# A graph attention layer with routed experts on one core: three expert tiles are turned by VectorE instead of TensorE, and the opening does its steps in another order

## The chip, the core and the metric

The kernel runs on one core of one Trainium2 chip. The core has five engines that each work through a queue of their own: TensorE (PE; its weight loads are listed apart as PEld), VectorE (DVE), ScalarE (ACT), GpSimd (POOL) and SyncE (SP), which here issues most of the transfers. Transfers themselves are moved by 16 DMA engines. Data lies in SBUF, products of TensorE land in PSUM banks, and inputs and outputs lie in device memory (HBM). The metric is device time in microseconds (us) for one run of the whole kernel. The median of three runs of the kernel before is 1252.25 us, from 1250.95 to 1253.42.

## The reference

All numbers are 32-bit floats; there are N = 4096 rows of D = 256 features, 4 heads of 64 columns, and 8 experts with 1024 hidden columns.

```python
def gnn(x, adj, W, a1, a2, Wr, br, gamma, beta):      # x is layernorm(x)
    h = einsum('nd,hdk->hnk', x, W)
    s_col = einsum('hnk,hk->hn', h, a1)
    s_row = einsum('hnk,hk->hn', h, a2)
    e = leaky_relu(s_row[:, :, None] + s_col[:, None, :], 0.2)
    att = softmax(where(adj > 0, e, -9e15), axis=-1)   # 4096 x 4096, four heads
    out = heads_side_by_side(einsum('hij,hjk->hik', att, h))
    y = elu(out) + x @ Wr + br
    return gamma * (y - mean(y)) / sqrt(var(y) + 1e-5) + beta

def ffn(x, Wg, bg, W1, b1, W2, b2):                    # x is layernorm(x)
    top_w, top_i = top_k(x @ Wg + bg, 2)
    share = softmax(top_w)                             # of the two experts chosen
    return sum(share[e] * (gelu(x @ W1[e] + b1[e]) @ W2[e] + b2[e])
               for the two experts e of each row)

x = x + gnn(layernorm(x), adj, ...)
x = x + ffn(layernorm(x), ...)
```

## The kernel before

**Attention.** Rows are held in blocks of 512 (four row tiles of 128 each). The attention runs over four row ranges of 1024 rows; in each, a loop over 32 column tiles `j` loads a tile of the transposed adjacency (`load_mask`), builds four heads' weights on VectorE (line 1703, tile `w`) and lets TensorE multiply them with the projected rows `ha` (line 1204, `acc`) and add them up (line 1213, `den`). In the first row range the projections of later blocks are made along the way.

**The opening** (`first_phase`, line 917) makes block 0 and 1 ready and starts the first columns while only the first half of the range is there. Its order is written out by hand: `in_trace_order` (line 819) ties every instruction to the one before it on its engine, so each engine works through the opening exactly in the order of the program text. Rows are centred on ScalarE (`centred`, line 839) from the means that `moments_of` (line 833) finds on VectorE, and are turned by TensorE, two row tiles at a time, in `turned_pair` (line 905: four transposes into one PSUM bank, then one copy to `turned[b]`). `weights_turned` (line 667) turns the heads' weights `wall` on TensorE and copies them on ScalarE to `wT`. `heads_made` (line 638) turns the vectors a1 and a2 on TensorE and spreads them on VectorE to `heads`. `scores_weights` (line 678) multiplies the two (`pw`) and copies the result into the last columns of `wall` (line 687), so that the projections `product_of` (line 897) give heads and scores at once. `squares_of_weights` and `limits_found` (lines 689 and 695) find a bound on the scores; `root_steps` (line 166) takes the inverse root of the variances in eleven short VectorE instructions. `rest_of_loads` (line 650) is seven loads issued by GpSimd, of which the first waits for the moments that it is given. `warm_up` (line 744) is matmuls on constants. All small PSUM results take turns in three banks (`bank`, line 245), and tiles of the tag `large` in three buffers.

**The experts.** During the attention of the later row ranges each finished row is routed: it is written, 260 floats wide (256 features, two shares, the row's number, the first choice), to the place of each of its two experts in `lists` in device memory. Expert tiles of up to 256 rows of one expert are then taken from these lists. The plan has 9 `early` and 8 `mid` tiles, which take rows of the first three row ranges, eight `final` ones with up to 512 rows, and two more; `todo` (line 2003) is their order. The main loop (line 2029) does for tile i, on TensorE in this order: the up products of tile i (`up`, line 1878, with gelu on ScalarE), a step of the last row block's own work (`between`, line 1989), the turn of tile i+1 (`turn`, line 1858), the down products of tile i (`down`, line 1900). The order on TensorE is fixed by `queue` (line 533). `fetch` (line 1791) issues on SyncE what a tile needs: rows, second bias, first and second weights (1 MB each, two buffers).

Rows come in one of two forms. The first NEAR tiles are **near**: `load_rows_of` (line 572) loads 256 whole rows of 260 floats in one transfer, ahead of time, and `turn_rows_of` (line 607) turns them with four TensorE transposes and two copies from PSUM. All others are loaded in **blocks**: `load_blocks_of` (line 583) issues one small transfer for the last four floats of each row (`known`) and eight for blocks of 32 rows by 32 columns, laid so that one VectorE instruction, which transposes every 32 by 32 block by itself (line 1871), gives the turned tile. Tile 0 is loaded and turned during the attention; tiles 1 to 5 have the buffers `early`.

The instructions' order in the queues outside of the hand-ordered parts is made by a planner that follows the program order, apart from what is ready much earlier.

Of the kernel before, what the change touches and what calls it, by code (L numbers as in the profile page):

```python
# [38 lines left out]
def over_partitions(vec, n):  # L39

    return bass.AP(tensor=vec.tensor, offset=vec.offset, ap=[[0, P], [1, n]])
# [3 lines left out]
def gat_then_moe(  # L45
# [19 lines left out]
    nc = tc.nc  # L65
    N, D = x.shape
    H, _, K = W.shape
    E, _, F = W1.shape
# [11 lines left out]
    MID = BOTH - EARLY  # L80
    LATE = 2 * N // TT - BOTH
    SURE = 2
    NEAR = 6
    KT = -(-N // TT)
    LAG = 6

# [2 lines left out]
    TB = B // P  # L89
# [76 lines left out]
    def root_steps(var, v, r, n, part=1.0, steps=3, sign=1):  # L166

        nc.vector.tensor_scalar(v, var, part, EPS, op0=OP.mult, op1=OP.add)
        yield
        nc.vector.tensor_scalar(  # L170
            r.bitcast(I32), v.bitcast(I32), -0.5, 1597463007.0, op0=OP.mult, op1=OP.add
        )
        yield
        for i in range(steps):
            way = sign if i + 1 == steps else 1
            q = small.tile([P, n], F32, tag="q", name="q")
            nc.vector.tensor_tensor(q, r, r, OP.mult)
            yield
            nc.vector.scalar_tensor_tensor(q, q, -0.5 * way, v, op0=OP.mult, op1=OP.mult)
            yield  # L180
            nc.vector.scalar_tensor_tensor(r, q, 1.5 * way, r, op0=OP.add, op1=OP.mult)
            yield
# [36 lines left out]
    def forward(apart, stack):  # L219
# [25 lines left out]
        def bank(shape, name):  # L245
            return ps.tile(shape, F32, tag="bank", name=name, bufs=3)
# [300 lines left out]
        def order_of(ins):  # L547

            if ordered[0] or strict[0]:
                queue(ins)  # L550
            return ins.ins
# [67 lines left out]
        with ExitStack() as layer:  # L619
# [30 lines left out]
            def rest_of_loads(behind=None):  # L650

                ins = nc.gpsimd.dma_start(wr, Wr.rearrange("(c p) d -> p c d", p=P)).ins
                if behind is not None:
                    after(ins, behind, "the first rows are loaded first")
                nc.gpsimd.dma_start(brm, over_partitions(br, D))
                nc.gpsimd.dma_start(wg[:, :, :E], Wg.rearrange("(c p) e -> p c e", p=P))
                nc.gpsimd.dma_start(bgb, over_partitions(bg, E))
                nc.gpsimd.dma_start(gam, over_partitions(gamma, D))
                nc.gpsimd.dma_start(bet, over_partitions(beta, D))
                nc.gpsimd.dma_start(b1r, b1.rearrange("e (c p) -> (e c) p", p=P))  # L660
# [6 lines left out]
            def weights_turned():  # L667

                pt = bank([P, 2, DC, P], "ptw")
                for i in range(2):  # L670
                    for c in range(DC):
                        order_of(nc.tensor.transpose(pt[:, i, c], wall[:, c, ts(i, P)], ident))
                wT = large("wT").rearrange("p t d -> p (t d)")[:, : 2 * DC * P]
                wT = wT.rearrange("p (i c d) -> p i c d", i=2, c=DC)
                nc.scalar.copy(wT, pt)
                return wT

            def scores_weights(wT):

                pw = bank([P, DC, 2 * H], "pw")  # L680
                for c in range(DC):
                    for i in range(2):
                        order_of(nc.tensor.matmul(
                            pw[:, c], wT[:, i, c], heads[:, i].rearrange("p s h -> p (s h)"),
                            start=(i == 0), stop=(i == 1),
                        ))
                nc.vector.tensor_copy(wall[:, :, HK:], pw)

            def squares_of_weights():

                sq = gat.tile([P, DC, H], F32)
                nc.vector.tensor_tensor(sq, wall[:, :, HK : HK + H], wall[:, :, HK : HK + H], OP.mult)
                return sq

            def limits_found(sq):

                pl = bank([P, H], "plim")
                for c in range(DC):
                    order_of(nc.tensor.matmul(
                        pl, all1f, sq[:, c, :], start=(c == 0), stop=(c == DC - 1)  # L700
                    ))
                v, r = (gat.tile([P, H], F32, name=name) for name in ("vlim", "rlim"))
                yield from root_steps(pl, v, r, H, 1.09 * D, steps=0)
                nc.vector.scalar_tensor_tensor(limits[:, :H], v, -1.0, r, op0=OP.mult, op1=OP.mult)
                yield
                nc.vector.tensor_tensor(limit, v, r, OP.mult)
                yield
# [125 lines left out]
            def moments_of(xb, mv, t):  # L833

                st = small.tile([P, 6], F32, tag="st", name="st")
                nc.vector.bn_stats(st, xb[:, t, :])
                return nc.vector.bn_aggr(mv[:, t, :], st).ins

            def centred(xb, mv, t):

                nc.scalar.activation(
                    xb[:, t, :], xb[:, t, :], AF.Identity, bias=mv[:, t, 0:1], scale=-1.0
                )
# [58 lines left out]
                        start=(c == 0), stop=(c == DC - 1),  # L902
                    ))

            def turned_pair(xb, b, t0, copy):

                pt = bank([P, DC, 2, P], "pt")
                for k in range(2):
                    for c in range(DC):
                        order_of(nc.tensor.transpose(pt[:, c, k], xb[:, t0 + k, ts(c, P)], ident))  # L910
                copy(turned[b][:, :, t0 * P : (t0 + 2) * P], pt.rearrange("p c k i -> p c (k i)"))

            def room_turned(b):
# [3 lines left out]
            def first_phase(weigh, norms):  # L917

                nc.scalar.activation(warm, tiny, AF.Exp)
                first = rows_loaded(0)  # L920
                mvs = [small.tile([P, TB, 2], F32, tag="mv", name="mv") for b in range(HB)]
                rs = [gat.tile([P, TB], F32, name=f"rrow{b}") for b in range(HB)]
                vs = [gat.tile([P, TB], F32, name=f"vrow{b}") for b in range(HB)]
# [3 lines left out]
                for t in range(2):  # L927
                    seen = moments_of(first, mvs[0], t)
                    centred(first, mvs[0], t)
                adj = load_adj(gat, range(R), 0, 1, 3)  # L930
                after(marks["adj"], seen, "the first rows and weights are loaded first")
                second = rows_loaded(1)
# [2 lines left out]
                    nc.sync.dma_start(first_adj[:, k], adjT[ts(2 + k, P), :R])  # L935
                fetched[2] = rows_loaded(2)
                room_turned(0)
                turned_pair(first, 0, 0, nc.vector.tensor_copy)
                wT = weights_turned()
                rest_of_loads(moments_of(first, mvs[0], 2))  # L940
                heads_made()
                warm_up(1)
                moments_of(first, mvs[0], 3)
                for t in range(2, TB):
                    centred(first, mvs[0], t)
                scores_weights(wT)
                turned_pair(first, 0, 2, nc.scalar.copy)
                sq = squares_of_weights()
                phs = [projected(t) for t in range(TB)]
                product_of(0, 0, phs[0])  # L950
                limit_steps = limits_found(sq)
                roots = root_steps(mvs[0][:, :, 1], vs[0], rs[0], TB, sign=-1)
                for _ in range(6):
                    next(roots)
                for _ in roots:
                    next(limit_steps, None)
                for _ in limit_steps:
                    pass
                for t in range(1, TB):
                    product_of(0, t, phs[t])  # L960
# [24 lines left out]
                roots = root_steps(mvs[1][:, :, 1], vs[1], rs[1], TB, sign=-1)  # L985
# [201 lines left out]
            def load_adj(pool, rows, j, n, bufs):  # L1187

                at = pool.tile([P, n, len(rows)], I32, tag="adj", name="adj", bufs=bufs)
                marks["adj"] = nc.sync.dma_start(  # L1190
                    at,
                    adjT[j * P : (j + n) * P, rows.start : rows.stop].rearrange(
                        "(t p) i -> p t i", p=P
                    ),
                ).ins
                return at
# [594 lines left out]
        def fetch(t, i):  # L1791
# [3 lines left out]
            chosen = t is early or t is mid  # L1795
            near = chosen and i + EARLY * (t is mid) < NEAR
            if near:
# [218 lines left out]
        def load_full(i):  # L2016
            xr = work.tile([CH, 2, RW], F32, tag="early", name="early", bufs=NEAR - 1)
            load_rows_of(early, i, xr)
            full_rows.append(xr)

        for i in range(1, NEAR):
            load_full(i)
            if i in (1, 4):
                jobs.append(fetch(*todo[len(jobs)]))
            if i in (1, 2):
                given.append(loads_of(b0 + i - 1, (residuals, large)[i - 1]))
# [64 lines left out]
    with tc.If(held(1, 1) > 0):  # L2091
        further()
        with tc.If(held(2, 1) > 0):
            with ExitStack() as again:
                held, further, rest_of_sums, _ = forward(False, again)
# [37 lines left out]
```

## Time and profile before

| | |
|---|---|
| median of three runs | 1252.25 us |
| the profiled execution | 1252.34 us |
| its span, first to last instruction | 1250.3 us |
| first weights of the attention (line 1703) begin | 16.6 us |
| attention's last product, first expert product | 775 us |
| expert tiles 0 to 5 | 775 to 862 us |
| last expert product ends | 1242 us |

The profile is of one execution. Times of instructions are counted from the start of the span. A row of a chain or a timeline gives the start, the duration, the engine, the tile that is written, the line, and how many instructions were joined; what stands in square brackets is the idle time of the engine before it and what ended it. Rows of a window give, after the stretch and its length, the busy time of TensorE, its weight loads, VectorE, ScalarE and GpSimd with the number of instructions in brackets, then TensorE's granted clock (1.00 is full), the busy share of the DMA engines, and GB/s. "SPq" is SyncE's queue issuing a transfer; the name of a line can be that of a helper.

### The profile page before, as it was taken

The numbers are of one execution on the slowest core, as the hardware profiler recorded it, in microseconds if no ns is written. First come the engines' busy times: TensorE is split into PE (matmuls) and PEld (weight loads), VectorE is DVE, ScalarE is ACT, GpSimd is POOL, SyncE is SP. The second block draws the span as 40 slices with busy tenths as digits, with TensorE's granted clock in tenths as the row PEclk, the third lists the DMA queues.
The fourth block names the chain that finished last, engine by engine and source line by source line (L and its number), as shares of the span: only waits on it lengthen the run. The fifth ranks groups of instructions, "written<-read, shape, count | busy, mean of one in ns | idle before, by whom it ended". The sixth has DMA issues, their size and how long they took to land.

```text
span 1250.3 us, 22717 instructions
## 1 busy us (share of the span) xinstructions
PE 1235.8 (99%) x8874; PEld 647.2 (52%) x8874; DVE 845.5 (68%) x1566; ACT 448.6 (36%) x918; POOL 242.1 (19%) x217
## 2 busy tenths in 40 slices
PE   9999999999999999999999999999999999999997
PEld 5444444332233332332324324888888876666686
DVE  6999887889999989999999996855111211111110
ACT  4332322165522375322655321533323332222322
POOL 4000000001002601006110015124432212222222
PEclk9999999999999999999999999999999999999999
DMA  6343433436533646335366322968889897555562
GB/s 216 107 131 118 158 114 102 145 126 147 177 113 105 224 116 202 104 101 157 115 164 199 119 81 100 274 167 228 218 244 250 193 234 149 109 135 114 133 164 31
DMA packets 155540, 190.22 MB, mean 152 GB/s; under 512 B 72312, under 2 KB 125680, under 8 KB 155040
## 3 DMA queue, kind: packets, MB, share of 16 engines
q1 hardware_dynamic: 133392, 145.39, 40.2%
q0 software_dynamic: 20544, 36.74, 13.3%
q10 hardware_dynamic: 1488, 6.55, 1.4%
q8 instruction: 71, 1.16, 0.4%
q14 instruction: 45, 0.37, 0.1%
HBM read 155.77 MB, written 29.74 MB: 148 GB/s over the span
## 4 chain that ended last, share of the span: by engine, by line
PE 94%; DVE 3%; issue 1%; DMA 1%; ACT 1%; POOLq 0%; SPq 0%; DVEq 0%; ACTq 0%
PE acc L1204 34%; PE po L1921 18%; PE ph L1887 17%; PE den L1213 17%; PE pr L1059 2%; DVE w L1703 2%; PE ph L1107 2%; PE acc L900 1%; PE ptx L1259 0%; DMA early<-lists 0%; PE pt L784 0%; PE ptr L1505 0%; PE po L1960 0%; PE pl L1270 0%; DMA xb<-in_x 0%
## 5 line engine op out<-in xcount | busy, mean ns | idle before, releaser
L1204 PE MATMUL acc<-w,ha 128*32 128x512 f32 x4096 | 669.7, 593 | 0.8 <-DVE w L1703 0.8
L1703 DVE SCALAR_TENSOR_TENSOR w<-er,eb,am 128x1024 f32<-128x1024 f32 x496 | 606.5, 1277 | 27.2 <-PE den L1213 27.2
L1213 PE MATMUL den<-w,unit 128*2 128x512 f32 x2048 | 466.5, 592 | 0.1
L1204 PEld LDWEIGHTS acc<-w,ha 128*32 128x32 f32 x4096 | 184.3, 110 | 291.4 <-issue 253.3
L1620 ACT ACTIVATE am<-adj 128x1024 bf16<-128x1024 int32 x124 | 130.7, 1054 | 352.5 <-DVE w L1703 194.3
L1887 PE MATMUL ph<-xT,w 128*128 128x256 f32 (+5 forms) x864 | 229.9, 423 | 0.2 <-ACT hT L1891 0.2
L1921 PE MATMUL po<-w,hT 128*128 128x256 f32 (+1 forms) x1040 | 229.7, 379 | 0.0
L1891 ACT ACTIVATE hT<-ph,bias 128x256 f32<-128x256 f32 (+5 forms) x216 | 111.4, 518 | 287.7 <-issue 181.6
L1921 PEld LDWEIGHTS po<-w,hT 128*128 128x128 f32 (+1 forms) x1040 | 195.7, 189 | 31.2 <-issue 3.4
L1887 PEld LDWEIGHTS ph<-xT,w 128*128 128x128 f32 x864 | 163.4, 190 | 59.8 <-issue 38.0
L1213 PEld LDWEIGHTS den<-w,unit 128*2 128x2 f32 x2048 | 93.6, 85 | 148.1 <-issue 139.1
L1946 POOL DMA_INDIRECT out<-o,ids x66 | 102.8, 1558 | 323.5 <-DMA out<-o,ids 144.1
L1934 DVE SCALAR_TENSOR_TENSOR o<-po,share,b2s 128x256 f32<-128x256 f32 (+2 forms) x66 | 31.6, 479 | 194.1 <-PE po L1921 167.5
L1390 POOL DMA_INDIRECT lists<-xe,at x64 | 89.2, 1394 | 267.3 <-issue 183.7
L1871 DVE STREAM_TRANSPOSE xT<-xr 128x512 f32<-128x512 f32 (+5 forms) x21 | 17.9, 851 | 87.5 <-DMA xr<-lists 42.3
L1059 PE MATMUL pr<-wr,xT 128*128 128x256 f32 x128 | 30.4, 381 | 0.2 <-ACT er L1153 0.2
L1909 ACT ACTIVATE b2s<-b2b,share 128x256 f32<-128x256 f32 x68 | 30.0, 498 | 0.0
L1127 POOL DMA_DIRECT2D residual<-rb x6 | 4.7, 786 | 122.1 <-DVE rb L1074 90.7
L1455 POOL DMA_DIRECT2D xf<-in_x x6 | 8.1, 1347 | 100.3 <-ACT xf L1454 100.3
L1059 PEld LDWEIGHTS pr<-wr,xT 128*128 128x128 f32 x128 | 24.1, 190 | 5.4 <-issue 0.9
L1107 PE MATMUL ph<-wall,xT 128*128 128x264 f32 x96 | 24.6, 399 | 0.0
L207 ACT ACTIVATE m<-y,off 128x256 f32<-128x256 f32 x48 | 23.7, 494 | 1.1 <-DVE off L215 0.6
(394 smaller groups left out, 617.3 us busy)
## 6 DMA issues: line engine op xcount, KB each, us to landing
adj<-in_adj SPq DMA_DIRECT2D x126, 512.0 KB
w<-in_L_ffn_W SPq DMA_DIRECT2D x54, 1024.0 KB
er<-parts ACTq DMA_DIRECT2D x3, 2048.0 KB
lists<-zeros POOLq DMA_DIRECT2D x8, 520.0 KB
residual<-rb POOLq DMA_DIRECT2D x8, 512.0 KB
rb<-residual SPq DMA_DIRECT2D x8, 512.0 KB
out<-y POOLq DMA_DIRECT2D x8, 512.0 KB
xb<-in_x SPq DMA_DIRECT2D x7, 512.0 KB
```

The source lines that it names most:

```text
L1059: order_of(nc.tensor.matmul(pr[:, k, :], turned[b][:, c, ts(t0 + k, P)], wr[:, c, :], start=(c == 0), stop=(c == DC - 1),))
L1107: order_of(nc.tensor.matmul(phs[t - t0], xT[:, c, ts(t, P)], wall[:, c, :], start=(c == 0), stop=(c == DC - 1),))
L1204: queue(nc.tensor.matmul(acc[half][h // 2][here : here + Q, :], ha[:, j, h * K + g * Q : h * K + (g + 1) * Q], w[half][h], start=(j == 0), ...
L1213: queue(nc.tensor.matmul(den[here : here + HB, :], unit[:, j, h, 1 - half : 1 - half + HB], w[half][h], start=(j == 0 and half == 0), stop ...
L1390: ins = nc.gpsimd.indirect_dma_start(lists, bass.IndirectOffsetOnAxis(ap=at[:, k, t : t + 1], axis=0), xe[:, t, :], None,).ins
L1620: nc.scalar.activation(am, at, AF.Relu, scale=2.0)
L1703: marks["w"] = nc.vector.scalar_tensor_tensor(wh[:, these], er[:, these, h], eb[:, j, h : h + 1], mask[:, these], op0=OP.max, op1=OP.min,).ins
L1887: order_of(nc.tensor.matmul(ph, job["w1"][:, c, ts(f, P)], xT[:, c, :], start=(c == 0), stop=(c == DC - 1),))
L1891: job["gelu"] = nc.scalar.activation(hT[:, f, :], ph, AF.Gelu, bias=job["bias"][:, f : f + 1]).ins
L1921: order_of(nc.tensor.matmul(po[:size], hT[:, f, k * CH : k * CH + size], w2[:, f, :], start=(f == 0), stop=(f == FC - 1),))
L1934: given_out.append(nc.vector.scalar_tensor_tensor(o[:size], po[:size], share[:size, k : k + 1], b2s[k][:size], op0=OP.mult, op1=OP.add,).ins)
L1946: added.append(add().ins)
```

## The change

Two parts. First, NEAR goes from 6 to 3: only tiles 0, 1 and 2 are near, and tiles 3, 4 and 5 come in blocks and are turned by VectorE like those behind them. The buffers `early` go from five to two, three row loads vanish, and the fetch of tile 2 moves ahead of the last block's second set of loads.

Second, the opening is put in another order. The heads' weights are turned ahead of the first pair of row tiles; the moments of row tiles 2 and 3 and the GpSimd loads come ahead of the adjacency loads in the text; `turned_pair` is split into `pair_turned` (TensorE) and `pair_kept` (the copy), so that the copy of the first pair comes behind `heads` on VectorE; two root steps follow it, and the other nine run behind the squares instead of between the steps of the limits.

```diff
-    NEAR = 6
+    NEAR = 3
...
+            def pair_turned(xb, b, t0):
                 pt = bank([P, DC, 2, P], "pt")
                 for k in range(2):
                     for c in range(DC):
                         order_of(nc.tensor.transpose(pt[:, c, k], xb[:, t0 + k, ts(c, P)], ident))
+                return pt
+
+            def turned_pair(xb, b, t0, copy):
+                pair_kept(pair_turned(xb, b, t0), b, t0, copy)
+
+            def pair_kept(pt, b, t0, copy):
                 copy(turned[b][:, :, t0 * P : (t0 + 2) * P], pt.rearrange("p c k i -> p c (k i)"))
...
                 for t in range(2):
                     seen = moments_of(first, mvs[0], t)
                     centred(first, mvs[0], t)
+                wT = weights_turned()
+                rest_of_loads(moments_of(first, mvs[0], 2))
+                moments_of(first, mvs[0], 3)
                 adj = load_adj(gat, range(R), 0, 1, 3)
                 after(marks["adj"], seen, "the first rows and weights are loaded first")
...
                 room_turned(0)
-                turned_pair(first, 0, 0, nc.vector.tensor_copy)
-                wT = weights_turned()
-                rest_of_loads(moments_of(first, mvs[0], 2))
+                for t in range(2, TB):
+                    centred(first, mvs[0], t)
+                pt = pair_turned(first, 0, 0)
                 heads_made()
                 warm_up(1)
-                moments_of(first, mvs[0], 3)
-                for t in range(2, TB):
-                    centred(first, mvs[0], t)
+                pair_kept(pt, 0, 0, nc.vector.tensor_copy)
+                roots = root_steps(mvs[0][:, :, 1], vs[0], rs[0], TB, sign=-1)
+                for _ in range(2):
+                    next(roots)
                 scores_weights(wT)
+                sq = squares_of_weights()
                 turned_pair(first, 0, 2, nc.scalar.copy)
-                sq = squares_of_weights()
                 phs = [projected(t) for t in range(TB)]
                 product_of(0, 0, phs[0])
-                limit_steps = limits_found(sq)
-                roots = root_steps(mvs[0][:, :, 1], vs[0], rs[0], TB, sign=-1)
-                for _ in range(6):
-                    next(roots)
                 for _ in roots:
-                    next(limit_steps, None)
-                for _ in limit_steps:
+                    pass
+                for _ in limits_found(sq):
                     pass
...
         for i in range(1, NEAR):
             load_full(i)
-            if i in (1, 4):
+            if i in (1, NEAR - 1):
                 jobs.append(fetch(*todo[len(jobs)]))
             if i in (1, 2):
                 given.append(loads_of(b0 + i - 1, (residuals, large)[i - 1]))
```

More of the change, by code (lines that the diff above doesn't have):

```diff
@@ L903, in product_of @@
                     ))
-            def turned_pair(xb, b, t0, copy):
+            def pair_turned(xb, b, t0):
                 pt = bank([P, DC, 2, P], "pt")
```

## The prediction

> **What bounds the kernel now.** I read the busy totals first, then the chain of waits, then windows of a few microseconds where TensorE is not full, then the DMA issue queue.
>
> ```profile
> PE 1235.8 (99%) x8874; PEld 647.2 (52%) x8874; DVE 845.5 (68%) x1566; ACT 448.6 (36%) x918; POOL 242.1 (19%) x217
> ```
>
> TensorE is busy 1235.8 of the span's 1250.3 us, so only two things shorten this kernel: less work on TensorE, or fewer of its 14.5 us of idleness. Windows of 5 us show the idleness in two places that the change touches, the first 15 us and 780 to 835 us; a third, the tail after 1242 us, is not touched. Elsewhere only about 1.2 us are lost (40 to 50, 650 to 655), so time won early is carried to the end.
>
> The chain of waits in the opening:
>
> ```profile
> 4.81 0.52 ACT xb L841
> 5.37 0.45 PE pt L910 x2
> 5.84 0.69 DVE xT L911
> 6.54 0.34 DVE st L836
> ...
> 7.00 0.17 DVE heads L644
> ...
> 7.31 1.03 PE pw L683 x8
> 8.34 0.64 PE pt L910 x4
> 8.98 1.76 PE acc L900 x4
> ```
>
> The heads' score weights (pw) wait for `heads`, and `heads` stands on VectorE behind the copy of the first turned pair (0.69 us) and the moments of row tile 2. The whole opening hangs on pw: its columns go into `wall`, which the first projection (L900) streams.
>
> One-microsecond windows of the same stretch (last columns: granted clock, DMA share, GB/s):
>
> ```profile
> 8.00:9.00 1.00, 1.00 (x9) 0.98 (x9) 0.55 (x4) 0.26 (x1) 1.00 (x3) 0.77 0.93 326
> 9.00:10.00 1.00, 1.00 (x3) 0.78 (x3) 0.83 (x6) 0.59 (x1) 1.00 (x3) 0.50 1.10 374
> ...
> 11.00:12.00 1.00, 1.00 (x4) 0.90 (x5) 0.58 (x7) 0.00 (x0) 0.62 (x2) 0.52 1.01 414
> ```
>
> The clock is halved from about 8.54 us (0.77 in that window is 0.54 full and 0.46 half) to about 11.96 us: 3.42 us long, while the projections run.
>
> The chain among the expert tiles, at the turns that go to VectorE (first and third shown):
>
> ```profile
> 815.64 0.50 ACT b2s L1909
> 816.14 0.49 ACT xT L1262
> 816.67 0.44 PE pt L611 x2
> 817.11 6.91 PE po L1921 x32
> ...
> 848.26 0.11 PE pg L1279
> 848.37 0.44 PE pt L611 x4
> 848.81 6.91 PE po L1921 x32
> ```
>
> A turn on TensorE costs its four transposes and, when the last row block's turns (L1259) hold the PSUM banks, a wait for ScalarE to empty one.
>
> **The change, expert tiles.** I count tiles from 0; the title's tiles 4 to 6 are my 3, 4 and 5. TensorE no longer transposes them.
> - Turn of tile 3, between tile 2's up and down products: the up products begin at 808.33 and take 6.91, so end at 815.24; the last block's eight transposes follow at 0.11 each, 0.88, to 816.12. The down products start at 817.11 now and can start at 816.12: 0.99 saved.
> - Turn of tile 4: up products from 824.59 end at 831.50; one gate transpose 0.11 and eight of 0.11 lead to 832.49. They now start at 833.57: 1.08 saved.
> - Turn of tile 5: only its four transposes stand in the way, 0.44.
>
> Sum 2.51 us. It can't be less than the twelve transposes at 0.11, 1.3 us, if the bank wait only moves to another instruction. Nothing else then holds the down products: the last gelu of tile 2 ends at 815.75.
>
> What is added, and what hides it:
>
> ```profile
> 841.98 6.03 SPq L595 DMA_DIRECT2D xr<-lists  x8
> ```
>
> - SyncE issues nine loads for each of the three tiles (one of 4 KB, eight of 32 KB) in place of one of 260 KB: 24 more. The eight took 6.03 us at tile 6, with the first about 6.6. SyncE's queue has room for them: after tile 2's second weight (792.04) until the bias load at 800.69, from 808.7 to 818.1, and from 824.4 to 834.6. Each set stands in `fetch` ahead of its own tile's bias and weights. If the first gap were gone, tile 3's first weight would slip from 801.6 by up to 6.6, and it is needed at about 822.5, so nothing is lost.
> - The second weight of tile 2 and the fetch around it pass the row loads of tiles 3 to 5 in SyncE's queue, and these vanish. The last block's own loads (x at 655, residual at 704) were already issued in the attention, so passing them changes nothing.
> - VectorE gets three stream transposes of 0.71 (2.1 us). It is nearly full from 790 to 823, but what it feeds there has slack: the last block's second half ends on it at 823.2 and TensorE takes that at 831.6, 8.4 us later. What waits behind a turn in VectorE's queue is that chain and the evacuation of the down sums, two PSUM banks ahead of TensorE.
> - ScalarE loses six copies of 0.37, none on the chain afterwards.
>
> [...] The blocks come in runs of 128. [...] The windows decide for hidden: the DMA engines are busy 0.49 in 810 to 820 and 0.49 in 830 to 840, ten microseconds of room, and tile 6's set, same shape, was being turned at 851.49, 9.5 us after its first issue, with 18 us left to its product at 869.74. I take 0.
>
> **The change, opening.** VectorE's order becomes moments of tiles 0 to 3, `heads`, the pair's copy, two root steps. TensorE's becomes the weights' transposes, the pair's, the a-vectors'.
> - Moments: the second pair ends at 4.77. Two more at 0.54 (their pitch in the second block, 19.45 to 20.01 to 20.54) plus gaps end at about 6.0, if the rows are there: data flow falls to 37 GB/s in 5 to 6 us, so all four row tiles and the weights have landed by about 5.2.
> - TensorE: pair done at about 5.85, the a-vectors at about 6.05. So `heads` runs from about 6.15 instead of 7.00. ScalarE copies the turned weights behind the second centring (5.32), by about 6.2 instead of 6.87.
> - pw starts near 6.5 instead of 7.31: 0.8 less. Late rows would make it 0.5; the ceiling is 0.9, since a-vectors and centring stay.
> - The pair's copy (0.69) and two root steps (0.2 each) end near 7.4, before pw ends at 7.5, so they cost nothing; the nine root steps left (1.8) run beside the first projection.
> - GpSimd's seven loads of weights and biases hang on tile 2's moments and go from about 5.7 instead of 7.38. They compete with the first adjacency load, which ScalarE wants at 13.3; covered. SyncE's loads keep their order and their wait for tile 1's moments. The turned weights now take a `large` buffer before the third block's rows do; both are free then.
>
> Now the clock. From 8.98 to 14.52 TensorE does 2.98/2 + 2.56 = 4.05 us of full-speed work. **By the row**, the half-speed stretch stays at 8.54 to 11.96: starting at 8.18, 0.36 is done before it, 1.71 in it, 1.98 after it, end 13.94: 0.58 saved. If the stretch moves along, 0.8. [...] I take 0.7, nearest the row.
>
> **Sum.** The profiled execution took 1252.34, 0.09 above the median of the runs. 1252.34 - 2.5 - 0.7 = 1249.1.
>
> **Rivals.**
> [...]
> - *One part pays, the other is given back.* The bank wait stays or the rows come late: between 1252.34 - 2.5 = 1249.8 and 1252.34 - 0.7 = 1251.6. The change not doing what it says ends here too: if row tile 3 landed only near 6.5 us, `heads` would stand as it does now.
> - *Slower: a turn blocks VectorE.* Its queue is in order. If tile 3's blocks, issued into DMA engines that are full until 798 (shares of 1.05 from 780 to 795), are late, everything behind the transpose waits. The later stage shows such waits:
>
> ```profile
> 895.92 0.71 DVE L1871 STREAM_TRANSPOSE xT<-xr 128x512 f32<-128x512 f32 x1 [1.43 <-DMA xr<-lists]
> ...
> 959.08 0.71 DVE L1871 STREAM_TRANSPOSE xT<-xr 128x512 f32<-128x512 f32 x1 [9.33 <-DMA xr<-lists]
> ```
>
>   TensorE feels it once VectorE stands longer than 8.4 - 0.7 = 7.7 us, and the kernel is slower than before from 7.7 + 3.2 = 10.9. One tile period late (16.3) gives 1249.1 + 8.6 = 1257.7. Against: at tile 6 the wait was 0.17, and the 9.33 came when blocks had streamed for seven tiles, with VectorE otherwise idle.
>
> **Chances.** Sum as worked out 0.52, clock up 0.13, one part only 0.22, slower 0.13. The range 1246.8 to 1252.2 leaves out the slower case and the lower edge of the clock's. About 0.2% (2.5 us, so below 1249.75) is what a measurement can tell from no change: three in four of the first case, all of the second and a little of the third lie there, 0.57 in all; within 0.2% 0.30; slower 0.13. The likeliest case alone spans 1248.0 to 1250.3.
>
> **What would show it.** Right: the transposes at L611's place number 12 rather than 24; the down products of tiles 2 and 3 follow the last block's transposes without a gap; stream transposes rise from 21 to 24; pw begins near 6.5; TensorE's busy time falls and its gaps after 15 us stay. Wrong: a stream transpose waiting over 8 us before 860, a new TensorE wait behind `xe` or `o`, `heads` still near 7, or a second half-clock stretch.

## The result

The changed kernel takes 1247.19 us (median of 7 runs, 1246.93 to 1249.43) against 1252.25 us for the kernel before (7 runs beside it, 1250.87 to 1253.42). The ratio is 0.9967, with a 95% interval of 0.9958 to 0.9976: 0.33% faster. The forecast was 1249.1 in a range of 1246.8 to 1252.2. The sign and the range held. The likeliest case was wrong in one step, and the kernel landed in the case that the chances call "clock up", which had been given 0.13.

One thing has to be known to read any time below: in some executions of this kernel the TensorE clock falls to half for a few microseconds in the opening and in others it doesn't, and a fall shows as a mean granted clock of 0.997 or less against 0.998 to 0.999 (the two profiled ones with a fall have 0.996 and 0.997; 3.41 us at half clock take 0.0014 off the mean clock over 1250 us).

The profiled execution of after took 1246.93 us with a span of 1245.2, against 1252.34 and 1250.3. Its totals, then the groups:

```profile
PE 1232.1 (99%) x8862; PEld 644.9 (52%) x8862; DVE 846.7 (68%) x1569; ACT 447.1 (36%) x912; POOL 240.7 (19%) x217
```

TensorE has 12 instructions fewer and is busy 3.7 us less. Its idleness went from 14.5 to 13.1 us. VectorE has its three additional instructions, ScalarE six fewer.

The opening, from the chain of waits of after (start, duration, what; the lines with "issue" are left out):

```profile
5.29 0.44 DVE st L836
...
5.76 0.18 DVE mv L837
5.94 0.32 DVE st L836
...
6.28 0.04 DVE mv L837
...
6.38 0.17 DVE heads L644
...
6.69 1.03 PE pw L683 x8
7.72 0.49 PE pt L910 x4
8.21 0.93 PE acc L900 x4
9.14 0.34 PE plim L699 x4
9.48 2.79 PE acc L900 x12
```

`heads` now stands behind the moments of row tile 3 alone, and the copy of the pair is gone from the chain. The score weights start at 6.69 instead of 7.31, which is 0.62 of the forecast 0.8. The larger thing is in the durations: four products of the first projection take 0.93 instead of 1.76. The last twelve end at 12.27, and in before at 14.52:

```profile
11.39 3.13 PE acc L900 x12
```

The one-microsecond windows of the same stretch, whose last three columns are the granted clock, the DMA share and GB/s, say why:

```profile
8.00:9.00 1.00, 1.00 (x7) 0.87 (x6) 0.85 (x6) 0.59 (x1) 1.00 (x3) 1.00 0.93 294
9.00:10.00 1.00, 1.00 (x8) 0.94 (x7) 0.84 (x6) 0.00 (x0) 1.00 (x3) 1.00 1.11 378
...
11.00:12.00 1.00, 1.00 (x6) 0.75 (x4) 0.23 (x1) 1.00 (x3) 0.00 (x0) 1.00 1.05 426
```

The clock is 1.00 where it was 0.77, 0.50 and 0.52. The record of before's granted clock has its changes in the opening at 5.13, 8.54 and 11.95 us, 3.41 apart; below and in the expectations such a stretch of 3.41 us is called a window, and where it lies is its phase. Of the 2.25 us won, 0.62 is the earlier start and 1.63 the clock. The attention's last product starts 2.25 earlier as well, so nothing is given back in the attention.

The turns of the expert tiles, from the chain of after:

```profile
799.10 6.91 PE po L1927 x32
806.01 6.91 PE ph L1893 x32
812.91 0.87 PE ptx L1265 x8
813.79 6.91 PE po L1927 x32
...
821.27 7.11 PE ph L1893 x32
828.37 0.11 PE pg L1285
828.48 0.87 PE ptx L1265 x8
829.36 6.91 PE po L1927 x32
...
836.95 7.10 PE ph L1893 x32
844.05 0.11 PE pg L1285
844.16 6.91 PE po L1927 x32
```

And from that of before, at the first and second turn:

```profile
801.42 6.91 PE po L1921 x32
...
824.59 7.12 PE ph L1887 x32
...
833.57 6.91 PE po L1921 x32
```

The four transposes of L611 are gone from the three turns, and so is the wait for ScalarE ahead of two of them; the down products follow the last block's own eight transposes (now L1265) without a gap. From one down product to the next, the distances were 15.69, 16.46 and 15.24 us before (801.42 to 817.11, 833.57, 848.81) and are 14.69, 15.57 and 14.80 now (799.10 to 813.79, 829.36, 844.16): 1.00, 0.89 and 0.44 saved, 2.33 in all.

What was added stays hidden. From SyncE's issues, and from VectorE in order of time (in brackets the idle time ahead of the instruction and what ended it):

```profile
791.26 6.30 SPq L595 DMA_DIRECT2D xr<-lists  x8
...
822.27 7.29 SPq L595 DMA_DIRECT2D xr<-lists  x8
```

```profile
802.19 0.71 DVE L1877 STREAM_TRANSPOSE xT<-xr 128x512 f32<-128x512 f32 x1 [0.21 <-DMA b2b<-in_L_ffn_b]
```

The transpose for tile 3 ends at 802.90, 18.4 us ahead of that tile's first product at 821.27, and no new TensorE wait appears between 765 and 900 us.

The sum closes. Opening: the last attention product starts at 772.72 instead of 774.97 and the first down product at 782.78 instead of 785.10, so 2.32. Turns 2.33. The stretch from the end of the last product to the end of the span is 7.8 instead of 8.25: 0.45. Outside the span 1.7 instead of 2.0: 0.3. Together 5.4, the difference of the two profiled executions.

### The profile page after: what moved, and what is told of

The parts are those of the page before. It is cut to its first block, busy times and chain, and to the rows that moved or that the text cites. A ratio compares the mean times of both kernels' runs of the same rounds, so it can differ in the third digit from the quotient of the medians.

```text
span 1245.2 us, 22780 instructions
## 1 busy us (share of the span) xinstructions
PE 1232.1 (99%) x8862; PEld 644.9 (52%) x8862; DVE 846.7 (68%) x1569; ACT 447.1 (36%) x912; POOL 240.7 (19%) x217
## 3 DMA queue, kind: packets, MB, share of 16 engines
q10 hardware_dynamic: 1488, 6.55, 1.4%
## 4 chain that ended last, share of the span: by engine, by line
PE 94%; DVE 3%; DMA 1%; issue 1%; ACT 0%; SPq 0%; POOLq 0%; DVEq 0%; ACTq 0%
PE acc L1210 34%; PE po L1927 18%; PE ph L1893 17%; PE den L1219 17%; PE pr L1065 2%; DVE w L1709 2%; PE ph L1113 2%; PE ptx L1265 1%; DMA early<-lists 0%; PE acc L900 0%; PE pt L784 0%; PE ptr L1511 0%; PE po L1966 0%; PE pl L1276 0%; DMA xb<-in_x 0%
```

## The experiments

The runs were made on three chips. The kernel before stands at 1251.38 (30 runs), 1251.13 (23) and 1252.0 (16) on them; every ratio is against the runs on the same chip.

**The tiles alone.** The kernel before with only the tiles' half of the change.

```
-    NEAR = 6
+    NEAR = 3
...
-            if i in (1, 4):
+            if i in (1, NEAR - 1):
```

> The opening as before, only tiles 3 to 5 in blocks. Theory (parts add up, the turns are worth what the chain showed): 2.4 us less than before, median near 1249.8, and the first attention weights (line 1703) start near 16.6 us as before. Rival (the turns' cost moves to another wait, all of the gain is the opening's): 1252.2, no change. The half-clock stretch of about 3.4 us in the opening stays in most runs, as before.

Measured: 1248.12 us (1247.58 to 1249.58, 9 runs), ratio 0.9974 (0.9964 to 0.9984). That is 3.3 less than before and not 2.4. The chain between the tiles has the same shape as in after:

```profile
814.10 0.87 PE ptx L1259 x8
814.97 6.91 PE po L1921 x32
```

The turns are worth the same without the new opening: the four down products start at 800.28, 814.97, 830.54 and 845.34, the same distances as in after. But in this profile the clock was up in the opening, although the opening was that of before (score weights at 7.44, first projection at 8.96). So with the old order the fall comes in some executions and not in others. Where the clock was up in both, the medians are 1248.04 (7 runs) and 1251.06 (19 runs): 3.0 us, which is 2.3 of turns, 0.45 at the tail and 0.3 not placed.

**The opening alone.** The kernel after with the tiles as before.

```
-    NEAR = 3
+    NEAR = 6
...
-            if i in (1, NEAR - 1):
+            if i in (1, 4):
```

> Only the opening changed, NEAR stays 6. Theory (heads' product 0.6 us earlier, and the clock not halved in the opening in most runs): 2.2 us less, median near 1250.0, first attention weights near 14.4 us, granted clock 1.00 in every microsecond from 8 to 12. Rival (the clock in the profiled run was luck of the window's phase, the order is worth 0.6 us alone): about 1251.6, and half-clock as often as before.

Measured: 1250.72 us (1249.96 to 1252.07, 13 runs), ratio 0.9993 (0.9985 to 1.0001), so the interval reaches no change. Of the theory the clock held (one fall in 13), of the rival the size: 0.66 us. With the clock up in both, 1250.72 (12 runs) against 1251.06, this half is worth 0.34 and the tiles' half 3.0, together somewhat less than the 3.6 to 3.8 of the whole change found below on other chips. In its profile the chain ahead of the score weights is another one:

```profile
4.86 0.91 PE ptw L672 x4
...
6.28 0.95 ACT xb L841 x2
7.23 1.01 PE pw L683 x8
```

Here the clock came up only at 6.56 us, so the transposes took 0.42 each and not 0.27, and the chain stands behind them: the score weights start at 7.2 with the same order as in after. So the 0.62 holds for one pair of executions. Where the clock came up at nearly the same moment (5.14 us with tile 2 in blocks, below, and 5.13 in before), the score weights start at 6.84 and 7.31: 0.47. Against the late one here it is 0.1.

**More or less work in the gap.** Both kernels hold one idle matmul (L748, 128x512, bf16) between the first transposes and the score weights, put there by `warm_up(1)`. Three in its place, in before and in after:

```
-                warm_up(1)
+                warm_up(3)
```

> The kernel before with three idle matmuls instead of one between the a-vectors' transpose and the heads' product, so that TensorE does more in the gap while nothing is moved ahead. Theory (the gap's thin work lets the clock fall, and the fall costs 1.7 us): the clock stays up in all runs or most, median 1250.6 to 1250.9, runs within 1 us of one another, heads' product still near 7.3 us. Rival (the clock falls by the window's phase whatever fills the gap): 1252.2, spread as before.

> The changed kernel with three idle matmuls instead of one in the same place. [...] Rival: the idle matmuls only delay the heads' product, up to 0.4 us, 1247.5, and a run near 1249.4 still comes now and then.

Measured: before with three 1250.99 us (1250.65 to 1251.27, 13 runs), ratio 0.9996 (0.9988 to 1.0004), and not one execution with a fallen clock; after with three 1247.52 (1247.0 to 1248.2, 6 runs), ratio 0.9969 (0.9957 to 0.9981), none fallen. In before, the fall can therefore be taken away by idle work alone, without any new order. That removes the long executions (the kernel beside it reached 1254.56) and moves the median by 0.4, to near the 1250.9 of the theory. In after no execution came near 1249.4, but the rival's delay is there too: the score weights start at 7.53, against 7.21 in a profile of the changed kernel whose clock also came up late ("after, again" below); the first projection starts only 0.1 later, at 8.81 against 8.72.

And none, in before:

```
-                warm_up(1)
```

> The kernel before without the idle matmul in the gap: TensorE does less there, nothing else is moved. Theory (thin work in the gap lets the clock fall, depending on the phase of a window): more runs with the low granted clock (0.995 to 0.997) than the 11 of 30 seen in the kernel before, more than half of them, median near 1252.3. Rival (the idle matmul is too small to count): the same share as before, median near 1251.4.

Measured: 1252.57 us (1250.93 to 1253.9, 12 runs), ratio 1.0001 (0.9992 to 1.0011). The clock fell in 8 of 12, and those took 1252.43 to 1253.9 against 1250.93 to 1251.43 for the others. In the profiled one it stayed up, so its chain says nothing of the fall; the count does.

**What in the order moves the heads.** Two kernels that each put one step of the new order back, beside the changed kernel itself on one chip. First the changed kernel again:

> The changed kernel itself, on one chip with the three variants beside it. Theory (what the change is worth with the clock up in both kernels is 3.9 us, and before loses the clock in a third of its executions): median 1247.2, 0.3% under before's median of about 1251.2, at most one execution in five above 1248.5. Rival (the 5.1 us between the two profiled executions is the worth, and the fall of the clock is no part of it): before's median near 1252.3 and the difference 5.

Measured: 1247.71 us (1247.28 to 1247.82, 5 runs), ratio 0.9964 (0.995 to 0.9978), no fall. On this chip before fell in 7 of 16 and has a median of 1251.3 where it didn't. With the clock up in both, the change is worth 3.6 here, and 3.8 in the first comparison (1247.16 against 1250.95). The medians as they stand differ by 4.3, because before fell more often here than the third that was expected. Its profile has the late phase that the opening alone had, `7.21 1.03 PE pw L683 x8` in its chain, 0.5 later than in the first profile of the same kernel.

Then the copy of the pair ahead of the heads:

```
+                    pair_kept(pt, 0, 0, nc.vector.tensor_copy)
                     heads_made()
                     warm_up(1)
-                    pair_kept(pt, 0, 0, nc.vector.tensor_copy)
```

> The changed kernel with one thing put back: the pair's copy stands ahead of the heads on VectorE. Theory (the copy's 0.69 us was what held the heads): heads start at about 6.95 instead of 6.38, the score weights at 7.25, the gap without thick matmuls grows to 3.9 us, so the clock falls in some executions; 1247.7 where it is up, 1249.3 where it falls. Rival (the moments or the a-vectors set the heads, the copy fits in an idle stretch before): heads within 0.15 us of 6.38, 1247.2.

Measured: 1249.66 us (1247.82 to 1251.42, 10 runs), ratio 0.998 (0.9971 to 0.999). The clock fell in 7 of 10 executions, and the profiled one shows a fall:

```profile
6.57 0.66 DVE xT L917
7.22 0.08 DVE heads L644
...
7.45 1.03 PE pw L683 x8
8.48 0.72 PE pt L910 x4
9.20 1.76 PE acc L900 x4
```

```profile
8.00:9.00 1.00, 1.00 (x10) 1.00 (x9) 0.41 (x3) 0.00 (x0) 1.00 (x2) 0.80 0.96 315
9.00:10.00 1.00, 1.00 (x4) 0.79 (x4) 0.82 (x6) 0.58 (x1) 1.00 (x3) 0.50 1.12 359
```

This experiment shows that the copy's place moves the heads, and the clock with them. A copy of 0.66 us, put back on VectorE, moves the score weights to 7.45 and the first projection to 9.20, about what it was before; the median rises by 1.95, three times the copy. The three executions without a fall took 1247.82 to 1248.59 (median 0.2 over the changed kernel's); the other seven 1249.38 to 1251.42. So most of what the copy costs comes by way of the clock.

Then the pair's transposes ahead of those of the heads' weights:

```
+                room_turned(0)
+                pt = pair_turned(first, 0, 0)
                 wT = weights_turned()
...
-                room_turned(0)
...
-                pt = pair_turned(first, 0, 0)
```

> The changed kernel with one thing put back: TensorE turns the first pair ahead of the heads' weights. Theory (the order on TensorE is worth nothing by itself, since the a-vectors come behind both): a-vectors and heads within 0.15 us, score weights within 0.2 us of the changed kernel's 6.69, time 1247.2. Rival (ScalarE's copy of the turned weights was the late one): the score weights 0.3 us or more later, waiting for that copy, and the time 0.3 us or more higher.

Measured: 1248.15 us (1247.53 to 1250.2, 7 runs), ratio 0.9971 (0.996 to 0.9982), one fall in seven. The score weights start at 6.99 and wait for `heads`, whose moments stand there behind row data that landed 0.3 later than in after. `heads` ends at 6.86, ScalarE's copy of the turned weights only 0.05 before it, at 6.81:

```profile
6.22 0.59 ACT L675 COPY wT<-ptw 128x512 f32<-128x512 f32 x1 [0.97 <-PE ptw L672]
```

In after this copy starts at 5.22 and `heads` ends at 6.55. With its rows as early as there, the copy would have been the last, so the rival of that expectation is not refuted: turning the weights first takes their copy off the path. The 0.4 between the medians is of the size by which the phase of the clock moves one profile of the changed kernel against another, so what this step is worth by itself stays open.

**Narrower loads.** The row blocks of tiles 3 to 5 in 16 loads of 16 columns in place of 8 of 32, so runs of 64 bytes.

```
-                    begun.append(nc.sync.dma_start(
-                        xb[ts(a, Q), c], rows[:, here : here + Q].rearrange("(k p) d -> p k d", p=Q)
...
+                    parts_of = 2 if t is early and i < 6 else 1
+                    wide = Q // parts_of
+                    for g in range(parts_of):
+                        begun.append(nc.sync.dma_start(
+                            xb[ts(a, Q), c, :, ts(g, wide)],
...
```

> The changed kernel with each block of tiles 3 to 5 loaded as two of 16 columns: 16 loads and runs of 64 bytes for each tile instead of 8 and 128, twice the cost that the forecast put at nothing. Theory (the blocks are hidden, some 16 to 20 us of slack): 1247.2 to 1248, as the changed kernel, the stream transposes a few us later and TensorE without a new wait. Rival (the loads are near their limit): SyncE's queue holds the weights back, TensorE waits, 1250 or more.

Measured: 1247.51 us (1247.29 to 1247.61, 5 runs), ratio 0.9964 (0.9951 to 0.9977). SyncE needs nearly twice as long for a set, and VectorE turns tile 3 4.5 us later:

```profile
792.14 11.04 SPq L598 DMA_DIRECT2D xr<-lists  x16
```

```profile
806.64 0.70 DVE L1883 STREAM_TRANSPOSE xT<-xr 128x512 f32<-128x512 f32 x1
```

Nothing of it reaches TensorE: tile 3's first product starts at 822.03, 14.7 us after the turn's end at 807.34, and every expert product from the first down product (783 us, before these loads) to the last comes 0.75 to 0.76 later than in after, an offset that was there before the loads. The cover under which the forecast had put the added loads holds even for the doubled cost.

**Further tiles in blocks.** Tile 2 too, and then tiles 1 and 2 (the loop that loads whole rows ends earlier).

```
-    NEAR = 3
+    NEAR = 2      (the second kernel: 1)
...
-        for i in range(1, NEAR):
-            load_full(i)
-            if i in (1, NEAR - 1):
-                jobs.append(fetch(*todo[len(jobs)]))
-            if i in (1, 2):
-                given.append(loads_of(b0 + i - 1, (residuals, large)[i - 1]))
+        for i in range(1, 3):
+            if i < NEAR:
+                load_full(i)
+            jobs.append(fetch(*todo[len(jobs)]))
+            given.append(loads_of(b0 + i - 1, (residuals, large)[i - 1]))
```

> The changed kernel with tile 2 in blocks too. Theory (a turn is worth its transposes and the bank wait behind them): the gap between tile 1's up and down products, 0.44 of transposes and 0.5 to 0.6 of waiting, goes: 0.9 less, about 1246.3. Rival (its blocks are issued into DMA engines that are full until 798 and come late, or VectorE's queue stands): no gain or a loss, 1247.2 to 1250.

Measured: 1246.78 us (1246.31 to 1247.07, 5 runs), ratio 0.9958 (0.9945 to 0.997). From its chain:

```profile
798.63 6.91 PE po L1927 x32
805.54 0.88 PE ph L1893 x4
...
806.48 1.28 ACT L1897
...
808.30 4.58 PE ph L1893 x20
812.89 0.87 PE ptx L1265 x8
813.76 6.91 PE po L1927 x32
```

The table load (line 1897) in this chain, with ScalarE in order of time, first in after and then here:

```profile
802.22 1.28 ACT L1897 ACT_TABLE_LOAD   x1
806.91 0.47 ACT L1897 ACTIVATE hT<-ph,bias 128x256 f32<-128x256 f32 x1 [3.40 <-PE ph L1893]
```

```profile
802.67 1.28 ACT L1570 ACT_TABLE_LOAD   x1 [3.61 <-DVE r L170]
...
806.48 1.28 ACT L1897 ACT_TABLE_LOAD   x1 [1.46 <-PE ph L1893]
```

The turn saves 1.19: from the first down product to the second it is 15.13 (783.50 to 798.63) instead of 16.32. But the down product after that comes 30.26 us after the first one instead of 31.01, which is only 0.75. Tile 2's up products now take 7.35 us (805.54 to 812.89) where they took 6.91, because the load of the gelu's table comes only behind the wait for the first of them, and TensorE, twelve products on, has to wait for a gelu. In after the same load ran at 802.22, beside tile 1's down product, and its 1.28 us cost nothing. A wait moved one tile on and took 0.44 with it.

On another chip, beside the changed kernel:

> Tile 2 in blocks as well, beside the changed kernel on one chip. Theory (1.2 us of turn saved, 0.4 to 0.5 given back to a load of the gelu's table that now falls into tile 2's up products): 0.4 to 0.7 us below the changed kernel, 1246.6. Rival (the 0.4 seen between two chips was the chip): the same as the changed kernel within 0.2 us.

Measured: 1246.93 us (1246.55 to 1250.3, 5 runs), ratio 0.9965 (0.9951 to 0.9978), against 1247.71 for the changed kernel. Four of the five lie between 1246.55 and 1247.07, below all five of the changed kernel; the fifth, 1250.3, has its clock up and a cause that was not found. In ratios to the kernel before (0.9965 and 0.9964) the two can't be told apart. In the two profiles of this chip the third down product comes 30.27 us after the first, against 31.01, so the 0.75 in this stretch is shown twice; of the whole time not more than some tenths of a microsecond is.

> The changed kernel with tiles 1 and 2 in blocks too, so that only tile 0 is turned by TensorE. Theory: another 0.9 to 1.2 us for tile 1's turn (0.88 of transposes and waits between 780 and 783), 1245.3. Rival (the blocks of tile 1 are wanted 15 us after they can first be issued, behind 3 MB of weights and with eight issues more ahead of them in SyncE's queue): TensorE waits for tile 1 or its weights, 1247 to 1252, slower than with tile 2 alone.

Measured: 1250.32 us (1248.67 to 1252.76, 12 runs), ratio 0.9988 (0.9978 to 0.9997). Most of the gain is given back. With the clock up the median is 1249.18 (7 runs), still 1.7 and 2.4 above the two kernels before it on the same chip (1247.51 and 1246.78). TensorE's longest waits from 850 to 1250 us, where after has none:

```profile
PE ph L1893 <- DVE xT L1877: 2.4, 1, 2.4
PE ph L1893 <- DMA w<-in_L_ffn_W: 2.0, 1, 2.0
```

At tile 1 nothing is lost. Its up products wait 0.6 for the last block's row chain on VectorE, but its down products come 24.42 us after the attention's last product (773.35 to 797.77), where after needs 26.38. The loss comes later: from 962 us TensorE waits for weights, and from 1019 us for rows that VectorE turned at 1020.53, after loads that SyncE issued from 1009.58 to 1019.26. Together they make 4.5 us, and the last expert product ends 5.06 later than in after. Why the queue is late there isn't shown: a set of eight loads takes 8.2 to 10.9 us in that stretch, and 8.7 to 10.8 in after. This profiled execution took 1252.0, 2.8 above the median with the clock up, so how much of the median such waits carry stays open too. In five executions the mean clock is 0.997 or 0.996; where it fell in them isn't known, and in the profiled one it stayed up through both waits. So tile 1 is the point where blocks stop being free, by a cost that comes some 170 us behind it.

## Why the prediction was right and where it failed

**The tiles, forecast 2.51, measured 2.33: right.** Turn by turn the forecast was 0.99, 1.08 and 0.44; it is 1.00, 0.89 and 0.44. The term that was mis-sized is the second. The forecast had let tile 3's up products take 6.91 us, "from 824.59 end at 831.50"; that is tile 2's figure. The row of before for tile 3 reads 7.12, and that of after 7.11. With it the same sum gives 1.08 - 0.2 = 0.88. The bank wait did not move to another instruction, so the lower bound of 1.3 was not needed.

**The covers: right.** SyncE's room, the DMA engines' room and the slack of VectorE all held, and the narrower loads show that SyncE's queue had as much again. The short runs of the blocks, 128 bytes each, were rightly given nothing at the end: with half the run length the time was 1247.51, and 1247.71 and 1247.19, on other chips, for the kernel as it is. The slower rival (1257.7) needed VectorE to stand 7.7 us; the transpose for tile 3 waited 0.21.

**The opening, forecast 0.7, measured 2.25 in the profiled execution: wrong, in the step "I take 0.7, nearest the row".** The first half of that step was nearly right: the score weights were forecast for 6.5 and came at 6.69, because the fourth moments ended at 6.3 and not at 6.0. The forecast's own figures give 6.3: rows landed by 5.2 (it was 5.27), and two moments of 0.54 behind them. The second half held the half-clock stretch fixed at 8.54 to 11.96 and let the work slide under it. The stretch isn't fixed to anything in the kernel. The record of the granted clock in the traces gives the moment at which it first comes up and any fall after it. (The rows of windows print 1.00 ahead of that moment; that TensorE is slower there shows in the transposes of 128x128, 0.42 us each ahead of it in "after, again" and 0.27 behind it in after.) The table has nine of the fourteen profiled executions; in the other five the clock comes up at 4.18, 4.68, 6.56, 6.64 and 7.13 and stays up:

| kernel (profiled execution) | clock up at, us | one window later | first projection at | clock then |
|---|---|---|---|---|
| before | 5.13 | 8.54 | 8.98 | falls 8.54 to 11.95 |
| copy ahead of heads | 5.19 | 8.60 | 9.20 | falls 8.60 to 12.01 |
| after | 4.35 | 7.76 | 8.21 | stays |
| after, tile 2 in blocks | 5.14 | 8.55 | 8.36 | stays |
| after, narrower loads | 4.84 | 8.25 | 8.40 | stays |
| pair's transposes first | 5.34 | 8.75 | 8.51 | stays |
| tiles alone (old order) | 5.66 | 9.07 | 8.96 | stays |
| before, no idle matmul | 6.08 | 9.49 | 8.99 | stays |
| after, again | 6.92 | 10.33 | 8.72 | stays |

In the traces of before, of the copy ahead of the heads and of after the changes lie whole multiples of 3.413 us apart (in before, 11.95 to the fall at 1244.16 behind the last product is 1232.21, or 361 times 3.4133; in after, 4.35 to the fall at 1239.97 behind the last product is 1235.62, or 362 times 3.4133). These windows aren't tied to the kernel's start: in the fourteen profiled executions the first rise lies between 4.18 and 7.13 us, with the same warm-up from 1.27 us. What in a window goes with a fall at its end shows only in part. In before's window from 5.13 to 8.54 TensorE was busy 2.73 us of 3.41 by the record, with transposes, eight-column products and one idle matmul, and the clock fell at its end all the same; in that of the copy ahead of the heads it was busy 2.45. The two windows that fell hold neither the end of the warm-up matmuls (4.86) nor the beginning of a projection, and all but one of those that stayed hold a part of one. The exception is the kernel with narrower loads, with 2.83 us busy and not 0.05 of either; and the kernel without the idle matmul stayed up with 2.61, but half a microsecond of that was projection. So neither busy time alone nor the thick products alone part the windows that fell from those that stayed, and what does isn't known.

What the forecast had to weigh was the length of the gap from the warm-up matmuls to the first projection, 4.1 us in before and 3.5 in after, against the 3.41 us of one window. It gave a clock that stays up 0.13, its author's own estimate: the one profile of before doesn't show how often the clock falls with a gap of either length. The counts below do. Thin work in the gap goes with the fall, and with the shorter gap the fall is rare: hardly any window fits into it any more. Counted over the executions:

| opening | idle matmuls in the gap | gap, us | clock fell in |
|---|---|---|---|
| before | 1 | 4.1 | 30 of 76 |
| before, with the new tiles | 1 | 4.1 | 2 of 9 |
| before | 0 | 4.1 | 8 of 12 |
| before | 3 | 4.0 | 0 of 13 |
| after, copy ahead of heads | 1 | 4.3 | 7 of 10 |
| after (six runs of four kernels with this opening) | 1 | 3.5 to 3.9 | 2 of 40 |
| after, pair's transposes first | 1 | 3.6 | 1 of 7 |
| after, tile 1 in blocks | 1 | 4.0 | 5 of 12 |
| after | 3 | 3.9 | 0 of 6 |

(Before's 76 are all its runs, the first seven of them sorted by their times. The gap runs to the first projection in the profiled executions. After's 3.9 is where the clock came up late, at 6.6 or 6.9, and then the window that begins there reaches well into the projections. The kernel with tile 1 in blocks has the opening of after too, and its clock came up late, at 7.13; whether its falls are in the opening isn't known, and if they are, they don't fit the 2 of 40.) Otherwise the order of the counts is that of the gap and of the idle matmuls. Their size isn't explained: of the phases of a window of 3.41 us, those that fit whole into a gap of 4.1 are 0.7 in 3.41, so 20%, and into one of 4.3 are 27%, while 39% and 70% fell. If the phase is evenly spread, the clock must sometimes fall after windows that touch thick work a little too; this wasn't shown.

**What the change is worth, then.** The 5.1 us of the medians holds an accident: four of before's seven executions had a fall, and so had the profiled one beside them, from which the forecast's sum starts. With the clock up in both kernels the change is worth 3.6 to 3.8, which is near the forecast's 3.2; with before falling in 30 of 76 executions, at 1.3 to 3.1 us between the medians of the two groups on the three chips, and after in 2 of 40, the rarity of the fall adds some 0.45 to 1.1 on average (an estimate from these counts). One window at half clock costs at most 1.7, half of 3.41, so the 3.1 of one chip needs more than one such window or something besides; no profile caught such an execution. Against that profiled execution the same sum with the measured 2.33 and 2.25 in it, 1247.8, would have been near, and the row it relied on was one throw of several. The measured time lies inside the range because the range was wide enough for a clock that stays up: 0.4 us above its lower edge.

**The tail, forecast untouched, measured 0.45 shorter.** It goes with the tiles' half: the last GpSimd scatter ends 4.85 to 4.93 us before the span does in the ten profiles with three or fewer tiles of whole rows, and 5.33 to 5.38 in the four with six. The records behind the scatter place it: GpSimd's semaphore ends 4.19 us behind the scatter in all of them, and the drain that follows ends 0.18 us after that in the ten and 0.64 in the four. Why that closing step is shorter wasn't found.

**"One part pays"** (0.22) didn't happen in the changed kernel: the bank wait is gone and `heads` came early. On its own the opening alone is not shown to pay by its ratio (0.9985 to 1.0001); with the clock up in both it is 0.34.

## What to carry to other kernels

Before costing an edit on a stretch with a halved clock, ask whether that stretch repeats from run to run: the spread of the times (here 1250.9 to 1253.4, two groups 1.5 us apart) shows it before any profile does, and one profiled execution is only one phase of it. Measure the gap between the dense matmuls on both sides of it against the window that the clock's own changes give (3.41 us here): closing it to about one window kept the clock up in 38 of 40 executions (51 of 59 with the two kernels listed apart), and two more idle matmuls in 19 of 19. And let each row give its own duration: the same 32 products took 6.91 us in one tile and 7.11 in the next.

## What was not expected of the hardware

- In before the clock fell to half behind a window (5.13 to 8.54) in which the record has TensorE busy for 2.73 of 3.41 us, with transposes, eight-column products and one idle matmul; with the copy ahead of the heads it fell behind one (5.19 to 8.60) with 2.45.
- The phase of these windows also moves what stands ahead of the projections: with the clock up at 4.35 us a transpose of 128x128 takes 0.27 us and the score weights start at 6.69; with the clock up at 6.92 it takes 0.42 and they start at 7.21, in the same kernel.
- Loads in runs of 64 bytes cost, here, SyncE's queue 11.0 to 11.7 us for a set of 16 (6.3 to 7.3 for 8 of 128 bytes) and TensorE nothing.
